# Layer 2's channel mixing: result copies on one engine, image 0 copied on chip, its first statistics split

## The chip, the cores and the metric

The kernel runs on one core of a Trainium2 chip. The metric is device time in microseconds; three runs of the kernel before gave 5497.55 to 5502.83, median 5501.04. TensorE (PE) multiplies matrices from SBUF into PSUM, VectorE (DVE), ScalarE (ACT) and GpSimd (POOL) work elementwise, and SyncE (SP) issues most of the transfers (DMAs). Each engine runs its own instructions in order, and engines wait for each other through semaphores.

## The reference

Four layers, each `x = x + f(norm(x))`, on 8 images of 56 x 56 positions and 192 channels. The change lies in layer 2, between its mixing and the layer norm behind it:

```python
proj = jnp.einsum('bhwd,dc->bhwc', x, W_in) + b_in           # 384 channels
local = depthwise 3x3 convolution of proj
lr, rl = ema_scan(local, 3), its mirror image                # s = 0.6 s + 0.4 x
tb, bt = ema_scan(local, 2), its mirror image
mixed = 0.25 * (lr + rl + tb + bt) + local
mu, var = mean and variance of mixed over the 384 channels
normed = (mixed - mu) * jax.lax.rsqrt(var + LN_EPS) * ln_g + ln_b
return jnp.einsum('bhwc,cd->bhwd', normed, W_out) + b_out
```

## The kernel before, in words

**Mixing** (`layer2_mix`, L1060 to L1153) runs over 24 groups of 16 channels, all 8 images at once. A group's convolution matrices `wt` and its inputs `zc` come from memory, two groups deep. Within a group the work goes in steps of four channels, with two halves:

- `front` (L1091): 16 matmul records on PE make the convolution in PSUM (`cv`, L1097, two buffers). ACT copies it to `loc` (L1105) and writes `rows`, the same with its two halves of partitions exchanged and scaled (L1108). POOL adds `loc` to `rows` (L1112). DVE makes the running sums along the image's height, downward (L1114) and upward (L1115), each a scan over 64 partitions. `loc` and `sums` have six buffers, `rows` three.
- `back` (L1120): 8 matmul records multiply `loc` and `sums` by a constant matrix (L1124), which adds the sums along the width, into PSUM (`mx`, two buffers of two halves). The first half of a buffer is copied into `yc` by DVE (L1133), the second by ACT (L1135).

A step works on the back half of one group and the front half of the next; the loop runs to 25 so that the last group's back halves stand alone at the end. When the four back halves of a group are done, SP stores `yc` for each of the 8 images into the image's buffer `md` in memory (L1151). For image 0, POOL then issues a load of the same channels back from `md[0]` into the tile `ml[0]` (L1152, called `first` there). `ml[0]` thus fills up during the mixing, while the other images are loaded whole later (`layer2_load`, L1155).

In this stage the order of instructions on each engine is chosen by the scheduler. It puts, on each engine, the back half of a step ahead of its front half: on DVE two scans and then the copy of an earlier product, on ACT the copy, then `loc` and `rows`. On SP the eight stores of a group stand ahead of the loads of a later one. From L1583 on, DVE's order is the written one.

**Behind the mixing** image 0 is normalised in groups of 8 columns of `ml[0]`, four of each half. `scaled(0, k, 0)` (L1588) takes the statistics of each column over the 384 channels (`ln_pieces`, bn_stats, L200), combines the two partial statistics into mean and variance with six small instructions (`ln_var`, L209 to L214), and makes scale and shift (`ln_rows`: a square root on ACT, L222, a reciprocal and a product on DVE, L223 and L224). `layer2_scaled` (L1160) applies them on DVE (L1167) and ACT (L1169), `layer2_turned` transposes on PE (L1178), `layer2_out` multiplies by `W_out` (L1191) and adds the residual tile `x2o` on DVE (L1196). While image 0 is worked on, SP loads the residuals (L101) and the mixed channels of image 1 (L1157), whose statistics DVE begins in the last third of image 0's work; these loads stand on SP behind the last group's stores.

Of the kernel before, what the change touches and what calls it, by code (L numbers as in the profile page):

```python
# [10 lines left out]
F32 = mybir.dt.float32  # L11
AF = mybir.ActivationFunctionType
ALU = mybir.AluOpType
# [4 lines left out]
B, H, W, C = 8, 56, 56, 192  # L18
# [24 lines left out]
C2 = 384  # L43
# [13 lines left out]
CG2 = 16  # L57
# [5 lines left out]
PH = NPAIR // 2  # L63
# [18 lines left out]
def _reversed(ap):  # L82

    dims = [list(d) for d in ap.ap]
    step, num = dims[-1]
    return bass.AP(ap.tensor, ap.offset + (num - 1) * step, dims[:-1] + [[-step, num]])
# [3 lines left out]
def kernel(ctx: ExitStack, tc: tile.TileContext, a: dict, out: bass.AP):  # L90
    nc = tc.nc
    nimg = a["x"].shape[0]
# [14 lines left out]
    def resident(name, eng=nc.sync, pool=const):  # L107
        t = pool.tile(list(a[name].shape), F32, name=name + "_sb", bufs=1)
        eng.dma_start(t, a[name])
        return t  # L110
# [10 lines left out]
    eps5 = const.tile([128, 1], F32, name="eps5")  # L121
# [28 lines left out]
    md = [dram.tile([2 * W, C2, NPAIR], F32, name=f"md{b}") for b in range(nimg)]  # L150
# [47 lines left out]
    def ln_pieces(st, yl, ns):  # L198
        for n in ns:
            nc.vector.bn_stats(st[:, n], yl[:, :, n])  # L200
# [13 lines left out]
        nc.vector.scalar_tensor_tensor(var, d, 0.25, var, ALU.mult, ALU.add)  # L214
        return mean, var

    def ln_rows(mean, var, eps, pool):

        P, A, n = var.shape
        new = lambda name: pool.tile([P, A, NPAIR // A], F32, name=name)[:, :, 0:n]  # L220
        rs, mr = new("ln_rs"), new("ln_mr")
        nc.scalar.activation(rs, var, AF.Sqrt, bias=eps[0:P])  # L222
        nc.vector.reciprocal(rs, rs)  # L223
        nc.vector.scalar_tensor_tensor(mr, mean, -0.5, rs, ALU.mult, ALU.mult)  # L224
        return rs, mr

    def in_quarters(st):
# [2 lines left out]
    def in_halves(st):  # L230
        return st.rearrange("p (s n) k -> p s n k", s=2)
# [543 lines left out]
    def layer1_norm(b, x, pool, psum, consts, first=False):  # L775
# [93 lines left out]
        for g in range(4):  # L869
            scaled(g)  # L870
            yield
# [189 lines left out]
    def layer2_mix(first):  # L1061

        band = a["band2"]
        with ExitStack() as st:
            pool = st.enter_context(tc.tile_pool(reuse_waits="tile", name="mx", bufs=2))
            psum = st.enter_context(tc.tile_pool(reuse_waits="tile", name="mxp", bufs=2, space=PSUM))
            ema = resident("ema", nc.gpsimd, pool)  # L1070
            NG = nimg * NPAIR
            dec = pool.tile([128, CG2 * nimg, NPAIR], F32, name="dec2", bufs=1)
            nc.gpsimd.memset(dec, 0.36)
            nc.gpsimd.memset(dec[:, :, 0:1], 0.0)
            dec = dec.rearrange("p c n -> p (c n)")

            def load(g):
                cs = slice(g * CG2, (g + 1) * CG2)
                wt = pool.tile([128, CG2, 256], F32, name="wt2")
                src = bass.AP(band.tensor, band.offset + g * CG2 * BL2, [[1, 128], [BL2, CG2], [1, 256]])  # L1080

                n, queues = (CG2, (nc.sync,)) if g else (4, (nc.sync, nc.gpsimd, nc.scalar))
                nc.sync.dma_start(wt[:, 0:n], src[:, 0:n])
                zc = pool.tile([128, nimg, CG2, P2], F32, name="zc2")
                for b in range(nimg):
                    queues[b % len(queues)].dma_start(zc[:, b], pd[b][:, cs])
                if n < CG2:
                    nc.sync.dma_start(wt[:, n:CG2], src[:, n:CG2])
                return wt, zc

            def front(c4, wt, zc):  # L1091

                ps = psum.tile([128, 2, 512], F32, name="cv2")
                for i in range(4):
                    dst = ps[:, i // 2, NG * (i % 2):NG * (i % 2 + 1)].rearrange("p (b n) -> p b n", n=NPAIR)
                    for q in range(2):
                        nc.tensor.matmul(  # L1097
                            dst, wt[:, c4 + i, 128 * q:128 * q + 128], zc[:, :, c4 + i, q:q + NPAIR],
                            start=(q == 0), stop=(q == 1),
                        )  # L1100
                loc, rows, sums = (
                    pool.tile([128, 4 * NG], F32, name=z, bufs=n) for z, n in (("loc", 6), ("rows", 3), ("sums", 6))
                )
                pair = lambda z: z.rearrange("p (j z) -> p j z", j=2)
                nc.scalar.copy(pair(loc), ps[:, :, 0:2 * NG])  # L1105

                for r in range(2):
                    nc.scalar.activation(  # L1108
                        pair(rows)[64 * r:64 * r + 64], ps[64 - 64 * r:128 - 64 * r, :, 0:2 * NG], AF.Identity,
                        scale=1.0 / 0.6,  # L1110
                    )
                nc.gpsimd.tensor_tensor(rows, rows, loc, ALU.add)  # L1112
                d = dec[:, 0:4 * NG]
                nc.vector.tensor_tensor_scan(sums[64:128], d[64:128], rows[64:128], 0.0, ALU.mult, ALU.add)  # L1114
                nc.vector.tensor_tensor_scan(  # L1115
                    _reversed(sums[0:64]), d[0:64], _reversed(rows[0:64]), 0.0, ALU.mult, ALU.add
                )
                return loc, sums

            def back(c4, yc, loc, sums):  # L1120
                ps = psum.tile([2 * W, 2, 512], F32, name="mx2")
                for i in range(2):
                    for k, z in enumerate((loc, sums)):
                        nc.tensor.matmul(  # L1124
                            ps[:, i, 0:2 * NG], ema[:, k],
                            z[:, 2 * NG * i:2 * NG * (i + 1)],
                            start=(k == 0), stop=(k == 1),
                        )
                for i in range(2):
                    src = ps[:, i, 0:2 * NG].rearrange("p (c b n) -> p b c n", c=2, n=NPAIR)  # L1130
                    dst = yc[:, :, c4 + 2 * i:c4 + 2 * i + 2]
                    if i == 0:
                        nc.vector.tensor_copy(dst, src)  # L1133
                    else:
                        nc.scalar.copy(dst, src)  # L1135


            loaded, now, n = [load(0)], None, C2 // CG2
            for g in range(n + 1):
                if g + 1 < n:  # L1140
                    loaded.append(load(g + 1))
                yc = pool.tile([2 * W, nimg, CG2, NPAIR], F32, name="yc2") if g else None
                following = []
                for c4 in range(0, CG2, 4):
                    if g:
                        back(c4, yc, *now.pop(0))
                    if g < n:
                        following.append(front(c4, *loaded[g]))
                if g:
                    for b in range(nimg):  # L1150
                        nc.sync.dma_start(md[b][:, (g - 1) * CG2:g * CG2], yc[:, b])  # L1151
                    nc.gpsimd.dma_start(first[:, (g - 1) * CG2:g * CG2], md[0][:, (g - 1) * CG2:g * CG2])  # L1152
                now = following  # L1153

    def layer2_load(b, pool):  # L1155
# [243 lines left out]
    with ExitStack() as st:  # L1399
        pool = st.enter_context(tc.tile_pool(reuse_waits="tile", name="qv", bufs=2))  # L1400
# [6 lines left out]
        rows, masks = [], []  # L1407
# [39 lines left out]
    with ExitStack() as st:  # L1447
        pool = st.enter_context(tc.tile_pool(reuse_waits="tile", name="mix", bufs=2))
# [24 lines left out]
    with ExitStack() as st:  # L1473
        pool = st.enter_context(tc.tile_pool(reuse_waits="tile", name="l1", bufs=2))
# [77 lines left out]
    with ExitStack() as st:  # L1552
        xpool = st.enter_context(tc.tile_pool(reuse_waits="tile", name="l2x", bufs=2, side="right"))
        pool = st.enter_context(tc.tile_pool(reuse_waits="tile", name="l2i", bufs=2))
# [16 lines left out]
    with ExitStack() as st:  # L1571
        mpool = st.enter_context(tc.tile_pool(reuse_waits="tile", name="l2m", bufs=1, side="right"))
        ml = [mpool.tile([2 * W, C2, NPAIR], F32, name="ml")]
        layer2_mix(ml[0])
        pool = st.enter_context(tc.tile_pool(reuse_waits="tile", name="l2o", bufs=2))
# [7 lines left out]
        st.enter_context(tc.manual_schedule(engines={mybir.EngineType.DVE}))  # L1583
        stat = lambda: pool.tile([2 * W, NPAIR, 6], F32, name="ln_st")
        rows, own, steps, ready, y = [None], stat(), iter(()), None, None

        def scaled(b, k, s):

            if b:
                return layer2_scaled(k, s, ml[b], *rows[0], 4 * k, pool)  # L1590
            if s == 0:
                ns = slice(4 * k, min(4 * k + 4, PH))
                ln_pieces(own, ml[0], [PH * r + n for r in range(2) for n in range(ns.start, ns.stop)])
                rows[0] = ln_rows(*ln_var(in_halves(own)[:, :, ns], C2, pool), eps5, pool)
            return layer2_scaled(k, s, ml[0], *rows[0], 0, pool)
# [5 lines left out]
        for n in range(-1, len(groups)):  # L1601
            b, k = groups[n] if n >= 0 else (-1, 0)
# [8 lines left out]
            for j in range(3):  # L1611
# [4 lines left out]
                if n >= 0:  # L1616
                    layer2_out(k, j, y, x[b], psum, w_out)
                    i = 3 * k + j
# [16 lines left out]
    with ExitStack() as st:  # L1635
# [5 lines left out]
        pool = st.enter_context(tc.tile_pool(reuse_waits="tile", name="l3o", bufs=2))  # L1641
# [135 lines left out]
```

## Time and profile before

| what | us |
|---|---|
| median of three runs | 5501.04 |
| profiled execution / its span | 5505.7 / 5503.9 |
| first convolution of the mixing | 3231.9 |
| last scan of the mixing begins | 3834.4 |
| last stores issued from | 3843.5 |
| first statistics of image 0 begin | 3850.3 |
| first scaled rows of image 0 begin | 3858.2 |

Mean durations in the mixing, in ns, with their number:

| instruction | count | mean |
|---|---|---|
| PE convolution cv, L1097 | 1536 | 355 |
| PE product mx from loc / from sums, L1124 | 384 / 384 | 553 / 544 |
| ACT loc, L1105 | 96 | 911 |
| ACT rows, L1108 | 192 | 912 |
| POOL addition, L1112 | 96 | 2326 |
| DVE scan, L1114 / L1115 | 96 / 96 | 2039 / 2901 |
| DVE copy, L1133 | 96 | 590 |
| ACT copy, L1135 | 96 | 532 |
| POOL issue of ml<-md, L1152 | 24 | 537 |

All times of the trace count from the start of the span. In lists of waits, "A <- B" means that A stood idle until B was done. Matmuls overlap, so the mean of one is longer than the distance to the next: two products of 448 columns start 0.75 us apart per pair. "PEld" is the load of weights into PE, which runs beside its matmuls.

### The profile page before, as it was taken

To read this page: it belongs to the slowest core of one execution; us is meant where nothing else is said; L and a number is where in the kernel's file an instruction comes from. 1 tells how busy PE (TensorE), PEld (TensorE's weight loads), DVE (VectorE), ACT (ScalarE), POOL (GpSimd) and SP (SyncE) were. 2 spreads that over 40 slices of the span, in tenths; PEclk is the share of its full clock that TensorE was granted. 3 is DMA by queue.
4 is the path that set the end of the run, shared out by engine and by line. 5 is a ranking of instruction groups with operands and counts; after the bars stand their busy time and mean duration, and the time that the engine had idled before them with its cause. 6 is when DMAs were issued, how large, how long until landed. Compare 5 with 4: busy or idle time off the path is not lost. (4 is left out here: it accounts for less than half of the span.)

```text
span 5503.9 us, 113538 instructions
## 1 busy us (share of the span) xinstructions
PE 4998.8 (91%) x49428; PEld 3379.9 (61%) x49428; DVE 3053.1 (55%) x4273; ACT 2311.1 (42%) x3109; POOL 1877.9 (34%) x1583
## 2 busy tenths in 40 slices
PE   7999969999999979999987989998798787999999
PEld 6778866666666645666665757775344586444444
DVE  4555533555555456666666868888777214343331
ACT  3444435555555434444441025554576302333333
POOL 5555555555555434344431023333011101001000
PEclk9999989999999989999998999999899898999999
DMA  5989896777777623223225757675777696212211
GB/s 148 234 222 232 222 269 261 272 273 275 277 276 272 201 68 85 77 81 86 82 59 156 270 214 235 230 237 188 182 218 220 241 340 235 65 61 87 70 40 27
DMA packets 533335, 1002.87 MB, mean 182 GB/s; under 512 B 256104, under 2 KB 467812, under 8 KB 501460
## 3 DMA queue, kind: packets, MB, share of 16 engines
q1 hardware_dynamic: 519984, 945.58, 53.5%
q0 software_dynamic: 8576, 40.69, 2.3%
q10 hardware_dynamic: 4276, 9.32, 0.6%
q8 instruction: 389, 6.37, 0.5%
q14 instruction: 110, 0.90, 0.1%
HBM read 665.22 MB, written 346.75 MB: 184 GB/s over the span
## 5 line engine op out<-in xcount | busy, mean ns | idle before, releaser
L465 POOL COPY lc<-lt 128x896 f32<-128x896 f32 (+1 forms) x320 | 616.4, 1934 | 513.9 <-PE op L473 490.7
L432 PE MATMUL qv<-w_qv_sb,x 64*112 64x256 f32 (+1 forms) x5376 | 692.0, 410 | 24.0 <-DVE act L438 20.1
L432 PEld LDWEIGHTS qv<-w_qv_sb,x 64*112 64x112 f32 x5376 | 592.5, 176 | 112.5 <-DVE act L438 32.2
L438 DVE TENSOR_TENSOR act<-qv,b_qv 112x640 f32<-112x640 f32 x448 | 318.7, 752 | 325.4 <-PE qv L432 238.5
L442 ACT ACTIVATE act<-act 112x640 f32<-112x640 f32 x448 | 300.3, 683 | 414.3 <-DVE act L438 403.7
L408 POOL TENSOR_TENSOR qv<-act 112x320 f32<-112x320 f32 x448 | 346.5, 799 | 288.9 <-ACT act L442 193.6
L473 PEld LDWEIGHTS op<-rc,lc 128*56 128x56 f32 x9216 | 329.6, 135 | 124.2 <-issue 65.9
L1366 PE MATMUL ph<-y,w_sb 64*128 64x392 f32 x2304 | 398.9, 499 | 6.5 <-ACT hid L1370 6.5
L473 PE MATMUL op<-rc,lc 128*56 128x56 f32 x9216 | 354.5, 221 | 55.1 <-ACT rc L465 38.2
L1377 PE MATMUL po<-hid,w_sb 128*64 128x392 f32 x2304 | 386.3, 494 | 0.0
L1384 DVE TENSOR_TENSOR x<-x,z 128x392 f32<-128x392 f32 x96 | 72.8, 759 | 520.3 <-ACT z L1382 520.3
L1097 PE MATMUL cv<-zc,wt 128*128 128x224 f32 x1536 | 312.8, 355 | 24.9 <-DMA zc<-pd 24.2
L1097 PEld LDWEIGHTS cv<-zc,wt 128*128 128x128 f32 x1536 | 290.3, 189 | 68.3 <-issue 53.1
L1366 PEld LDWEIGHTS ph<-y,w_sb 64*128 64x128 f32 x2304 | 220.7, 189 | 176.5 <-issue 26.5
L506 PE MATMUL y<-pp,w_o_sb 128*64 128x392 f32 x1536 | 309.0, 499 | 5.8 <-DVE pp L500 5.8
L1112 POOL TENSOR_TENSOR rows<-rows,loc 128x896 f32<-128x896 f32 x96 | 223.3, 2326 | 261.9 <-ACT rows L1108 204.6
L483 PE MATMUL pj<-xn,w_p_sb 64*128 64x392 f32 x1536 | 289.1, 509 | 19.7 <-ACT pp L490 18.1
L924 POOL TENSOR_TENSOR e<-e,mx 128x1176 f32<-128x1176 f32 x64 | 140.2, 2190 | 462.6 <-DVE mx L923 398.3
L465 ACT COPY rc<-rt 128x896 f32<-128x896 f32 (+1 forms) x160 | 279.9, 1749 | 40.0 <-DMA rt<-right 40.0
L1377 PEld LDWEIGHTS po<-hid,w_sb 128*64 128x64 f32 x2304 | 162.7, 137 | 213.8 <-issue 213.8
L500 DVE TENSOR_TENSOR pp<-pp,ot 128x784 f32<-128x784 f32 x128 | 124.1, 970 | 292.6 <-PE ot L495 239.9
L1115 DVE TENSOR_TENSOR_SCAN sums<-dec,rows 64x896 f32<-64x896 f32 x96 | 278.5, 2901 | 1.3
(252 smaller groups left out, 9194.8 us busy)
## 6 DMA issues: line engine op xcount, KB each, us to landing
lt<-left SPq DMA_DIRECT2D x72, 1792.0 KB
rt<-right SPq DMA_DIRECT2D x72, 1792.0 KB
left<-qv SPq DMA_DIRECT2D x224, 252.0 KB
right<-qv SPq DMA_DIRECT2D x96, 504.0 KB
wt<-in_band_dram SPq DMA_DIRECT2D x23, 2048.0 KB
zc<-pd SPq DMA_DIRECT2D x187, 232.0 KB
pd<-pt SPq DMA_DIRECT2D x7, 5568.0 KB
bm<-bmask SPq DMA_DIRECT2D x64, 588.0 KB
```

The source lines that it names most:

```text
L408: nc.gpsimd.tensor_tensor(qv[:, s, s0:s1, k], *(acts[s][:, which, 0:n].rearrange("p (s d) -> p s d", d=64) for which in range(2)), ALU.mult,)
L432: nc.tensor.matmul(ps[s][:, which, 0:n], x[64 * s:64 * s + 64, j, bass.ts(i, 2 * W)], w_qv[64 * s:64 * s + 64, j, which, 64 * s0:64 * s1], ...
L438: nc.vector.tensor_tensor(acts[s][:, :, 0:n], ps[s][:, :, 0:n], b_qv[:, :, 64 * s0:64 * s1], ALU.add)
L442: nc.scalar.activation(acts[s][:, :, 0:n], acts[s][:, :, 0:n], AF.Silu)
L465: copy(c[:, 0:nu], raw.rearrange("p (w u d) -> p u d w", u=nu, d=64 // nu)[:, :, d0:d0 + 8])
L473: nc.tensor.matmul(op[64 * u:64 * u + W, i, :], lc[:, u, i], rc[:, u, i], start=True, stop=True)
L483: nc.tensor.matmul(ps[:, s, 0:TT], w_p[64 * s:64 * s + 64, j, 128 * c:128 * c + 128], xn[64 * s:64 * s + 64, j, bass.ts(t, TT)], start=(j ...
L506: nc.tensor.matmul(y[64 * s:64 * s + 64], w_o[:, 2 * g + u, 64 * j:64 * j + 64], pp[:, u, s], start=(u == 0), stop=(u == 1),)
L1097: nc.tensor.matmul(dst, wt[:, c4 + i, 128 * q:128 * q + 128], zc[:, :, c4 + i, q:q + NPAIR], start=(q == 0), stop=(q == 1),)
L1115: nc.vector.tensor_tensor_scan(_reversed(sums[0:64]), d[0:64], _reversed(rows[0:64]), 0.0, ALU.mult, ALU.add)
L1366: nc.tensor.matmul(ps[:, s, 0:TT], w0[64 * s:64 * s + 64, j, m * 128:(m + 1) * 128], y[64 * s:64 * s + 64, j, ts], start=(j == 0), stop=(j ...
L1377: nc.tensor.matmul(ps[64 * s:64 * s + 64], w1[:, m, 64 * j:64 * j + 64], hid[:, m, s], start=(m == 0), stop=(m == 5),)
```

## The change

Both halves of a result are copied out of PSUM by ACT; DVE's copy is gone. For image 0, SP transfers the channels from `yc` straight into `ml[0]`, ahead of the seven stores of the other images; `md[0]` and POOL's load are no longer used. The statistics of image 0's first 8 columns are taken in two parts: over the first 368 channels as soon as DVE has done its last scan and those channels are there, and over the last 16 channels once they have arrived; bn_aggr combines both parts of a column. It gives the mean itself, not twice the mean, and so `ln_rows` has a factor to be given. The other columns are handled as before.

```diff
-    def ln_rows(mean, var, eps, pool):
+    def ln_rows(mean, var, eps, pool, share=-0.5):
...
-        nc.vector.scalar_tensor_tensor(mr, mean, -0.5, rs, ALU.mult, ALU.mult)
+        nc.vector.scalar_tensor_tensor(mr, mean, share, rs, ALU.mult, ALU.mult)
...
                 for i in range(2):
                     src = ps[:, i, 0:2 * NG].rearrange("p (c b n) -> p b c n", c=2, n=NPAIR)
-                    dst = yc[:, :, c4 + 2 * i:c4 + 2 * i + 2]
-                    if i == 0:
-                        nc.vector.tensor_copy(dst, src)
-                    else:
-                        nc.scalar.copy(dst, src)
+                    nc.scalar.copy(yc[:, :, c4 + 2 * i:c4 + 2 * i + 2], src)
...
                 if g:
-                    for b in range(nimg):
+                    nc.sync.dma_start(first[:, (g - 1) * CG2:g * CG2], yc[:, 0])
+                    for b in range(1, nimg):
                         nc.sync.dma_start(md[b][:, (g - 1) * CG2:g * CG2], yc[:, b])
-                    nc.gpsimd.dma_start(first[:, (g - 1) * CG2:g * CG2], md[0][:, (g - 1) * CG2:g * CG2])
...
+        early = pool.tile([2 * W, 8, 12], F32, name="ln_early", bufs=1)
+        for n in range(8):
+            nc.vector.bn_stats(early[:, n, 0:6], ml[0][:, 0:C2 - CG2, PH * (n // 4) + n % 4])
...
-            if s == 0:
+            if s == 0 and k == 0:
+                for n in range(8):
+                    nc.vector.bn_stats(early[:, n, 6:12], ml[0][:, C2 - CG2:C2, PH * (n // 4) + n % 4])
+                both = pool.tile([2 * W, 2, 4, 2], F32, name="ln_mv", bufs=1)
+                for n in range(8):
+                    nc.vector.bn_aggr(both[:, n // 4, n % 4], early[:, n])
+                rows[0] = ln_rows(both[:, :, :, 0], both[:, :, :, 1], eps5, pool, -1.0)
+            elif s == 0:
```

## The prediction

> **What bounds the kernel now.** I read the page first, then the chain that ended last, then the stretches of the mixing stage, its waits, and the instructions in order of time. On the page TensorE is the busy engine of the whole program, and the chain that ended last walks through this stage's end:
>
> ```profile
> PE 4998.8 (91%) x49428; PEld 3379.9 (61%) x49428; DVE 3053.1 (55%) x4273; ACT 2311.1 (42%) x3109; POOL 1877.9 (34%) x1583
> ```
>
> The mixing stage runs from about 3220 to 3859 us. Busy time by stretch (us of PE, PEld, DVE, ACT, POOL, then granted clock, DMA share, GB/s) shows two different regimes:
>
> ```profile
> 3300.00:3800.00 500.00, 497.88 (x1931) 352.74 (x1930) 437.12 (x241) 254.22 (x322) 196.72 (x101) 1.00 0.70 233
> 3800.00:3837.00 37.00, 31.77 (x107) 19.61 (x106) 32.61 (x21) 16.44 (x22) 12.05 (x7) 0.95 0.30 98
> 3837.00:3859.00 22.00, 4.74 (x8) 1.91 (x8) 9.00 (x20) 2.59 (x5) 6.64 (x7) 0.66 0.67 175
> ```
>
> For 500 us PE is full and VectorE (DVE) 87% full; then come 22 us in which PE works 4.7. The chain names what fills those 22 us (start, length, what):
>
> ```profile
> 3837.50 4.75 PE mx L1124 x8
> 3843.49 2.19 DMA md<-yc
> 3846.22 3.97 DMA ml<-md
> 3850.26 6.14 DVE ln_st L200 x8
> 3858.23 2.67 ACT yt L1169 x3
> ```
>
> Everything here is in series: last product, one transfer out, one back, eight statistics, first scaled rows.
>
> A busy PE can still lose time. The waits of 3300 to 3800 (us in total, times, longest):
>
> ```profile
> ACT yc L1135 <- DVE yc L1133: 240.8, 80, 5.7
> PEld mx L1124 <- ACT yc L1135: 12.8, 34, 1.4
> ```
>
> and two steps (a step is four channels of convolution and four of result):
>
> ```profile
> 3503.04 0.59 DVE L1133 COPY yc<-mx 112x448 f32<-112x448 f32 x1
> 3503.67 0.53 ACT L1135 COPY yc<-mx 112x448 f32<-112x448 f32 x1 [4.63 <-DVE yc L1133]
> 3504.25 1.01 PE L1124 MATMUL mx<-loc,ema_sb 128*112 128x448 f32 x2
> 3507.35 3.24 PE L1097 MATMUL cv<-zc,wt 128*128 128x224 f32 x16
> 3510.43 0.91 PE L1124 MATMUL mx<-loc,ema_sb 128*112 128x448 f32 x2
> 3511.59 2.08 POOL L1112 TENSOR_TENSOR rows<-rows,loc 128x896 f32<-128x896 f32 x1 [1.99 <-ACT rows L1108]
> 3511.67 3.87 DVE L1115 TENSOR_TENSOR_SCAN sums<-dec,rows 64x896 f32<-64x896 f32 x1
> 3513.43 3.24 PE L1097 MATMUL cv<-zc,wt 128*128 128x224 f32 x16
> 3516.09 2.02 DVE L1114 TENSOR_TENSOR_SCAN sums<-dec,rows 64x896 f32<-64x896 f32 x1
> 3519.77 3.24 PE L1097 MATMUL cv<-zc,wt 128*128 128x224 f32 x16
> ```
>
> The convolutions start 6.08 us apart, then 6.34. In the long step the product at 3504.25 had to wait until ScalarE's copy freed its PSUM buffer (there are two), and that copy stood behind DVE's copy, which stood behind two scans. So PE alone needs 6.08 us a step, and the copy chain adds 0.25 to every other one.
>
> **The change, part by part.** The order of instructions on PE is unchanged. On DVE 96 copies go, on ScalarE 96 come, on GpSimd (POOL) 24 DMA issues go, and on SyncE (SP) the first of each group's eight stores goes to the tile instead of memory. Only the first statistics block behind the stage differs beyond that.
>
> *Copies to ScalarE, long stretch.* ScalarE gains 96 x 0.53 us: 254 busy us of 500 become about 297, 3.8 us of a step. Queued behind its two copies are loc (0.91) and the two rows (1.83), and POOL and the scans wait for those. The two copies (1.06) fit beside the convolution (3.1 us), loc and rows beside the next product (3.0 us), so I cost them at nothing; without that cover each would add its 0.53 to the step. DVE loses 0.59 a step. With the copy no longer behind the scans, the PSUM wait of PE goes. From the convolution at 3250.55 to the last at 3817.62 there are 91 steps in 567.1 us; at 6.08 they would take 553.3, an excess of 13.8. The first of these steps (7.51 instead of 6.08, it waits for sums) keeps its 1.4, so at most 12.4 can go. The surely attributed part is about 35 waits x 0.25 = 8.8. I take 10.
>
> What is late next is the pair DVE and POOL. A step then holds two scans and one POOL addition, and they get in each other's way: the scan that starts 0.08 after the addition takes 3.87 instead of 2.02. In the trace that makes 2.04 + 3.87 = 5.9 us a step, under 6.08; while the stage fills, where they collide all the time, addition plus scan repeat every 3.75 us, so 3.75 + 2.04 = 5.8. The Trainium skill, "SBUF — State Buffer" (SBUF: two separate sides), speaks against the change: a DVE instruction with two SBUF inputs and a GpSimd one that reads SBUF exclude each other for the whole instruction. By that the step would be 2.08 + 2 x 2.04 = 6.16 us and only (6.23 - 6.16) x 90 = 6 us could go. The rows show about 0.2 to 0.3 us of each collision overlapped, so I follow the rows: PE stays the bound.
>
> *The tail.* Durations of before, from the last convolution at 3817.62: it ends 3820.86; loc and rows 2.8, to 3823.7; POOL 2.1, to 3825.85; two scans 4.1, to 3829.95 (before, 3836.37, since each of these engines was one or two steps behind the copies). PE meanwhile finishes the earlier products without waiting; the last one, 8 matmuls at 0.375, ends at 3832.95 (before 3842.2). Two copies on ScalarE in a row, 1.1: 3834.05. Before, the first store was issued at 3843.49: 9.4 us are gone.
>
> *Copy on chip.* The trace has no SBUF to SBUF transfer. Nearest is md<-yc of the same 196 KB: issued 3843.49, waiter free at 3846.22, 2.7 us. Bounds: 2.2 (its own piece in the chain) and 6.7 (both legs, no gain). I take 2.7: landed 3836.75. The leg ml<-md, 4.0 us, is gone. SP's number of issues is the same; behind the first stand seven stores. POOL loses 24 issues of 0.54 and the waits ahead of them, off the path; behind the last of them stood the load of w_out and a 4.6 us clearing of zq, which now come earlier than they are needed (before, w_out was issued at 3846.77 and first used at 3863.5).
>
> *Statistics in two parts.* Eight early bn_stats take 6.1 us as before (they read 368 of 384 channels). They wait for the transfers of groups 0 to 22, the last issued near 3819, and stand behind the last scan: 3829.95 to 3836.1. The gap between that scan and the last landing is 6.8, so they are hidden; uncovered they would cost up to 6.1. Then eight bn_stats of 16 values: small DVE instructions here take 0.09 to 0.20 each, so 0.7 to 1.6, taken 1.2. Eight bn_aggr of 12 values: from 0.1 each (a small instruction) to 0.47 (the row of bn_aggr of 72 values), 0.8 to 3.8; nearer the small ones, taken 2.4. Six small instructions of the old variance go, 1.0. Square root, reciprocal and shift stay, 0.8. First scaled rows: 3836.75 + 1.2 + 2.4 + 0.8 = 3841.2, before 3858.23: 17.0 earlier.
>
> *What is late next.* Image 0's residual and image 1's mixed channels are loaded by SP behind the stores, so they come only 9.4 us earlier, plus about 1 for the transfers taken out of the way. By the trace's DMA packets they were complete near 3864 and 3884; DVE first used them at 3870.98 and 3889.26. They now land near 3854 and 3873.5 and are wanted at 3854 and 3872.3. So 1.3 us come back, and the tail is worth about 15.5.
>
> Sum: 10 + 15.5 = 25.5 us. The profiled execution took 5505.7 (span 5503.9), so it would take about 5480; the median of the three runs is 5501.04, 0.08% below it, so 5475.5.
>
> **The rivals.**
> 1. *The port paces the long stretch* (17%). For it: that the scan nearly doubles in a collision, and that every step would now collide instead of every second. Against: 5.9 is below 6.08. The stretch gives 0 to 6 and the tail 15.5: about 5483.
> 2. *Everything comes* (10%). The loads do not hold image 0 up and PE keeps its full clock there (before, it was granted half speed from 3858 to 3878, after the idle stretch): 12 + 18: 5470.
> 3. *Little comes* (8%). The on-chip transfer is no faster than the two legs, the early statistics are not covered, or the copies hold ScalarE up: the tail gives 9, the stretch nothing: 5492.
> 4. *Slower* (5%). Both scans of each step are stretched by POOL, as in the filling of the stage (3.73 and 3.75). A step of 7.5 us would add 1.3 x 90 = 115 us: near 5600. It decides from a step of about 6.4 us (0.17 x 90 = 15.5, the tail's gain). Against it: one addition a step can stretch only one scan.
>
> That the change doesn't do what it says is not among them: on each engine the instruction order shows the moves.
>
> **How the numbers follow.** My forecast has 60% and covers 5469 to 5484; the likeliest value is 5475.5. To hold 8 in 10 the range takes in rivals 1 and 2: 5466 to 5489. A measurement of this kernel tells about 0.2%, 11 us, from no change. Faster by more: 60 + 17 + 10 and a third of rival 3, 90%. Same 5%, slower 5%.
>
> **What would show it.** Convolution starts all 6.08 apart and no PE wait for ScalarE's copy (stretch right); 6.16 or more with PE idle is rival 1. Last scan to first scaled rows about 11 us instead of 22. The transfer ml<-yc 2 to 3 us. Statistics: no wait of early ones, eight aggregates about 2.4. After it, a DVE wait of 1 to 2 us for image 1's channels. The forecast is wrong if the step stays at 6.2, or if image 0 waits for its loads by more than 5 us.

## The result, and the profile after

Six runs of the changed kernel gave 5469.26 to 5481.53 us, median 5473.73; six of the kernel before had a median of 5501.48. The ratio is 0.9949 (95% interval 0.9936 to 0.9962), so about 28 us are gone, 21 to 35 by the interval. The profiled execution took 5471.44 us, its span 5469.3: 34 us less than the profiled one of before. Some 8 of those 34 lie ahead of the mixing (its fifth convolution starts at 3242.57 instead of 3250.55), where nothing was changed; kernels that are equal up to there differ by as much (3238.66 in e4_no_early, 3251.20 in e5_no_chip). So I count from that convolution on.

The page's first line, and the busy time by stretch (columns as before: us of PE, PEld, DVE, ACT, POOL, then granted clock, DMA share, GB/s):

```profile
PE 4981.5 (91%) x49428; PEld 3382.6 (62%) x49428; DVE 2944.8 (54%) x4187; ACT 2362.1 (43%) x3205; POOL 1872.9 (34%) x1559
```

```profile
3300.00:3800.00 500.00, 500.00 (x1977) 363.83 (x1976) 346.24 (x167) 303.11 (x410) 190.17 (x83) 1.00 0.67 221
...
3837.00:3859.00 22.00, 16.53 (x70) 6.59 (x69) 13.54 (x26) 8.37 (x11) 0.00 (x0) 0.84 0.95 220
```

PE was full before and is full now, but the 500 us hold 1977 matmul records instead of 1931. That is how a gain shows on an engine that is "full": more records in the same time. VectorE (DVE) is busy 91 us less there (some 47 for its 80 copies, the rest because its scans are shorter, as shown below), ScalarE (ACT) 49 us more. The last stretch, nearly empty before, now holds work of image 0. The waits of 3300 to 3800 (us in total, times, longest):

```profile
POOL rows L1112 <- ACT rows L1108: 307.7, 82, 4.0
ACT loc L1105 <- PE cv L1097: 172.9, 82, 2.1
DVE sums L1114 <- POOL rows L1112: 152.4, 76, 2.0
ACT yc L1131 <- PE mx L1124: 20.8, 82, 0.3
```

No PE wait for a copy is left; everybody waits for PE, directly or one after the other. A step in order of time:

```profile
3499.62 0.97 ACT L1131 COPY yc<-mx 112x448 f32<-112x448 f32 x2 [0.25 <-PE mx L1124]
...
3501.61 2.02 DVE L1114 TENSOR_TENSOR_SCAN sums<-dec,rows 64x896 f32<-64x896 f32 x1 [2.02 <-POOL rows L1112]
...
3503.62 1.83 ACT L1108 ACTIVATE rows<-cv 64x896 f32<-64x896 f32 x2
3503.65 2.02 DVE L1115 TENSOR_TENSOR_SCAN sums<-dec,rows 64x896 f32<-64x896 f32 x1
...
3505.51 3.24 PE L1097 MATMUL cv<-zc,wt 128*128 128x224 f32 x16
3505.58 2.08 POOL L1112 TENSOR_TENSOR rows<-rows,loc 128x896 f32<-128x896 f32 x1 [4.01 <-ACT rows L1108]
...
3511.59 2.67 PE L1097 MATMUL cv<-zc,wt 128*128 128x224 f32 x13
```

Steps are 6.08 us, every one but the first (7.51, as before). And POOL's addition lies between the scans: it meets only the last 0.09 us of a second scan, and the next first scan begins when it is done. Now the tail:

```profile
3797.43 3.24 PE L1097 MATMUL cv<-zc,wt 128*128 128x224 f32 x16
...
3809.79 5.95 DVE L1584 BATCH_NORM_STATS2 ln_early<-ml 112x6 f32<-112x368 f32 x8
3813.72 0.52 SPq L1146 DMA_DIRECT2D ml<-yc  x1
3816.78 0.80 DVE L1592 BATCH_NORM_STATS2 ln_early<-ml 112x6 f32<-112x16 f32 x8 [1.04 <-DMA ml<-yc]
3817.49 0.70 DVE L1595 BATCH_NORM_AGGREGATE ln_mv<-ln_early 112x2 f32<-112x12 f32 x8
3819.05 3.07 ACT L1165 ACTIVATE yt<-ml,ln_mr,ln_rs 112x384 f32<-112x384 f32 x3 [0.52 <-DMA md<-yc]
```

Between the last convolution and the first scaled rows (`yt`) lie 21.62 us. Before there were 40.61, from the line below to the first scaled rows at 3858.23:

```profile
3817.62 3.24 PE L1097 MATMUL cv<-zc,wt 128*128 128x224 f32 x16
```

(The releaser that the line of 3819.05 names is a store; by the times it is the product of L224, done at 3818.97.)

The chain that ended last has left this path:

```profile
3800.67 12.04 PE mx L1124 x32
...
3819.07 0.68 SPq L101
...
3820.62 35.14 DMA ml<-md
3855.78 3.16 DVE ln_st L200 x4
```

It now runs through SP's queue and the load of image 1's channels, issued at 3820.62 behind the last stores and the first loads of image 0's residual. DVE wants these channels 4.5 us before they are there, and it waits as long for something else before that. Its first residual addition, and its first statistics of image 1:

```profile
3835.17 0.68 DVE L1192 SCALAR_TENSOR_TENSOR x2o<-po,vecs_sb,x2o 128x448 f32<-128x448 f32 x1 [4.51 <-PE po L1187]
...
3855.78 3.16 DVE L200 BATCH_NORM_STATS2 ln_st<-ml 112x6 f32<-112x384 f32 x4 [4.50 <-DMA ml<-md]
```

The first of these waits is put down to the product `po`, which was ready sooner: PE's ten products before it ended at 3830.57, and in e4_no_early the addition follows these ten at once. In e0_after_again, the same kernel once more, it is put down to image 0's residual:

```profile
3838.85 0.68 DVE L1192 SCALAR_TENSOR_TENSOR x2o<-po,vecs_sb,x2o 128x448 f32<-128x448 f32 x1 [3.48 <-DMA x2o<-x]
```

In the trace of after, too, the residual's second load reports its end at 3835.04, just ahead of the addition. So image 0 waits for two loads that stand behind the last stores: 4.5 us for its residual and 4.5 for image 1's channels (3.5 and 5.6 in e0_after_again).

### The profile page after: what moved, and what is told of

The parts are those of the page before. It is cut to its first block, busy times and chain, and to the rows that moved or that the text cites. A ratio compares the mean times of both kernels' runs of the same rounds, so it can differ in the third digit from the quotient of the medians.

```text
span 5469.3 us, 113665 instructions
## 1 busy us (share of the span) xinstructions
PE 4981.5 (91%) x49428; PEld 3382.6 (62%) x49428; DVE 2944.8 (54%) x4187; ACT 2362.1 (43%) x3205; POOL 1872.9 (34%) x1559
## 3 DMA queue, kind: packets, MB, share of 16 engines
q1 hardware_dynamic: 519984, 945.58, 53.9%
## 4 chain that ended last, share of the span: by engine, by line
PE 73%; DVE 11%; ACT 5%; DMA 4%; issue 3%; POOL 2%; SPq 1%; ACTq 0%; DVEq 0%; POOLq 0%
PE qv L432 10%; PE po L1373 7%; PE ph L1362 7%; PE mx L1124 5%; PE cv L1097 5%; PE pj L483 5%; PE pin L1044 4%; PE y L506 4%; PE qk_ps L886 4%; PE op L473 3%; PE po L1187 3%; PE v_ps L901 3%; PE cps L1265 3%; DVE ln_st L200 2%; PE ot L495 2%
## 5 line engine op out<-in xcount | busy, mean ns | idle before, releaser
L1362 PEld LDWEIGHTS ph<-y,w_sb 64*128 64x128 f32 x2304 | 220.4, 189 | 176.4 <-issue 26.1
L1114 DVE TENSOR_TENSOR_SCAN sums<-dec,rows 64x896 f32<-64x896 f32 x96 | 206.1, 2147 | 188.7 <-POOL rows L1112 188.1
```

Source lines behind the costliest of these rows:

```text
L1362: nc.tensor.matmul(ps[:, s, 0:TT], w0[64 * s:64 * s + 64, j, m * 128:(m + 1) * 128], y[64 * s:64 * s + 64, j, ts], start=(j == 0), stop=(j ...
```

## The experiments

My theory (A): the copies give the stretch and most of the tail; the copy on chip and the early statistics make image 0 start sooner, but image 1's load, tied to the last store, then holds image 0's end, so that they give little. The rival (B): the three parts add up.

For every run I took three times from its trace: the stretch (fifth to last convolution, 91 steps), the tail (last convolution to the first scaled rows) and image 0 (from these to its last residual addition). Their sum is free of what differs upstream; but it comes from one trace of each kernel, and it leaves out what follows image 0 (from there to image 7's last addition all these kernels take 386.9 to 388.9 us, e6_residual_early 390.8). The runs were made on several chips; each ratio is to the kernel before on the same chip.

| run | median us | ratio to before (interval) | stretch | tail | image 0 | sum, against before |
|---|---|---|---|---|---|---|
| before | 5501.48 | | 567.07 | 40.61 | 71.28 | 678.96 |
| after | 5473.73 | 0.9949 (0.9936–0.9962) | 554.86 | 21.62 | 76.49 | -26.0 |
| e0_after_again | 5475.36 | 0.9954 (0.9942–0.9966) | 554.86 | 21.60 | 76.47 | -26.0 |
| e1_scalar_only | 5476.18 | 0.9967 (0.9955–0.9980) | 554.87 | 31.01 | 70.44 | -22.6 |
| e2_chip_only | 5494.86 | 0.9996 (0.9987–1.0004) | 565.85 | 36.58 | 70.82 | -5.7 |
| e3_early_only | 5495.83 | 0.9999 (0.9990–1.0009) | 565.49 | 33.09 | 73.06 | -7.3 |
| e4_no_early | 5469.63 | 0.9948 (0.9936–0.9960) | 554.86 | 27.65 | 70.34 | -26.1 |
| e5_no_chip | 5476.64 | 0.9954 (0.9941–0.9967) | 554.86 | 25.66 | 72.21 | -26.2 |
| e6_residual_early | 5471.47 | 0.9951 (0.9939–0.9963) | 554.87 | 22.66 | 73.11 | -28.3 |
| e8_vector_copies | 5493.65 (one run; before, once there, 5491.67) | | 565.25 | 28.44 | 72.36 | -12.9 |
| e9_swapped | 5576.03 | 1.0142 (1.0128–1.0156) | 645.60 | 40.53 | 71.49 | +78.7 |
| e10_after_swapped | 5487.67 | 0.9977 (0.9968–0.9987) | 562.29 | 30.19 | 72.43 | -14.0 |

**One part alone.** e1_scalar_only is the kernel before with both copies on ACT:

```diff
-                    dst = yc[:, :, c4 + 2 * i:c4 + 2 * i + 2]
-                    if i == 0:
-                        nc.vector.tensor_copy(dst, src)
-                    else:
-                        nc.scalar.copy(dst, src)
+                    nc.scalar.copy(yc[:, :, c4 + 2 * i:c4 + 2 * i + 2], src)
```

> The kernel before with only the copies moved to ScalarE. By the chip of the first four runs and the trace of the changed kernel: the long stretch gives 12.2 us (steps of 6.08 instead of 6.23), the last copy ends 9.6 us sooner after the last convolution, and nothing behind it changes, so image 1's channels are not waited for: 21.8 us faster than the kernel before, some 4 us short of the changed kernel. If instead POOL's DMA issues hold the long stretch up as well, steps stay above 6.08 and the gain is under 15 us.

Measured: 554.87 for the stretch and 9.6 off the tail, 22.6 of the 26.0 us. Channels still travel through memory, POOL still issues its loads, and the stretch is the same to 0.01 us: those issues cost it nothing here.

e2_chip_only has only the transfer from `yc`, e3_early_only only the two-part statistics; each leaves the copies as before:

```diff
-                    for b in range(nimg):
+                    nc.sync.dma_start(first[:, (g - 1) * CG2:g * CG2], yc[:, 0])
+                    for b in range(1, nimg):
                         nc.sync.dma_start(md[b][:, (g - 1) * CG2:g * CG2], yc[:, b])
-                    nc.gpsimd.dma_start(first[:, (g - 1) * CG2:g * CG2], md[0][:, (g - 1) * CG2:g * CG2])
```

> The kernel before with only the copy on chip. If the long stretch is held up by the copy chain alone: steps stay at 6.2 us and the tail is shorter by the leg taken out, 3.7 us in all. If POOL's issues and its waits for the stores matter for the stretch: steps between 6.08 and 6.2, up to 12 us more.

> The kernel before with only the split statistics. Eight early ones fit into the 7.4 us in which DVE waited for the transfer, so the first scaled rows come 5.7 us sooner; before, image 1's channels landed about 5 us ahead of their use, so all of it but 0.5 stays: 5 us faster. If those channels land later than I read from the packets, DVE waits for them and less is left.

Measured: both shorten the tail (by 4.0 and 7.5) and leave the steps, the odd first one apart, at 6.20 us each (before 6.22). The timed runs can't tell either from before; the intervals reach from 7 us faster to 2 slower, and from 5 faster to 5 slower. The 7.3 us that e3_early_only gains in the table are more than its timed runs allow; the table is good for which part does what, not for a microsecond or two. So the stretch belongs to the copies alone.

**One part undone.** e4_no_early is the kernel after with the old statistics, e5_no_chip the kernel after with stores and POOL loads of image 0 as before; e0_after_again is the kernel after once more, beside them.

```diff
e4_no_early
-        early = pool.tile([2 * W, 8, 12], F32, name="ln_early", bufs=1)
-        for n in range(8):
-            nc.vector.bn_stats(early[:, n, 0:6], ml[0][:, 0:C2 - CG2, PH * (n // 4) + n % 4])
...
-            if s == 0 and k == 0:
...
-            elif s == 0:
+            if s == 0:
```

> The changed kernel with the statistics of image 0's first columns taken in one piece again (copies on ScalarE and the copy on chip stay). Its own gain in the trace: from the first late statistics to the first scaled rows 2.3 us instead of 8.0, so 5.7. Theory A, image 1's channels cap the tail: those loads are tied to the last store, so the 5.7 us are spent waiting for them, and without the early statistics the program takes the same time as the changed kernel (within 1.5 us), with DVE's wait for image 1's channels going from about 5.7 to about 0. Rival B, the parts add up: 5.7 us slower than the changed kernel, and the wait for image 1's channels stays.

> The changed kernel with image 0's channels stored to memory and loaded back by POOL again (copies on ScalarE and the split statistics stay). The leg taken out is worth 3.7 us in the trace (last store to first statistics 6.8 us before, 3.1 after). Theory A, capped by image 1's loads: same time as the changed kernel within 1.5 us, the wait for image 1's channels shrinking from about 5.7 to about 2. Rival B, the parts add up: 3.7 us slower. Rival C, POOL's DMA issues were part of what held the long stretch up: a step longer than 6.08 us in the long stretch, each 0.1 us being 9 us.

> The changed kernel once more, on the chip of the three others, as their measure: 0.9949 of the kernel before (0.9936 to 0.9962).

Measured: without the early statistics the tail is 6.0 longer and image 0 is 6.2 shorter; without the copy on chip the tail is 4.0 longer and image 0 4.3 shorter. The sums agree within 0.3 us and the three medians within 7 us, with intervals that overlap. In e4_no_early DVE waits for neither load. So by these traces each part adds about 3.5 us to e1_scalar_only and both together no more: B falls, A stands, though image 1's load is not alone in it. Against e4_no_early, image 0 of the kernel after loses 6.2 us: 1.7 by its fourth residual addition, behind the wait for the residual, and 4.5 at image 1's load.

**Take the cap away.** e6_residual_early is the kernel after with image 0's residual loaded during the mixing, so that image 1's load follows the last stores directly in SP's queue (room for it comes from a shorter `dec` and one `loc` buffer less). The lines that time this load and give the later residuals one buffer each are left out here:

```diff
-            dec = pool.tile([128, CG2 * nimg, NPAIR], F32, name="dec2", bufs=1)
+            dec = pool.tile([128, 4 * nimg, NPAIR], F32, name="dec2", bufs=1)
...
-                    pool.tile([128, 4 * NG], F32, name=z, bufs=n) for z, n in (("loc", 6), ("rows", 3), ("sums", 6))
+                    pool.tile([128, 4 * NG], F32, name=z, bufs=n) for z, n in (("loc", 5), ("rows", 3), ("sums", 6))
...
+                if g == 6:
+                    residual(following[-1][0][:, 0:1])
```

> The changed kernel with image 0's residual (2.4 MB) loaded during the mixing, in about the seventh group, instead of behind the last stores; to make room the scans' constant tile is a quarter as long and loc has five buffers. Theory A: image 1's channels then stand first behind the stores and land 8 us earlier, so the wait of about 5.7 us for them goes and the program is about 5 us faster than the changed kernel (near 5468 where that takes 5473). Rival B: they do not set the end; no change within 1.5 us. Either way up to 2 us can be lost in the group in which the residual is loaded.

Measured: DVE's waits for both loads are gone, as wanted, but most of the gain is not there. Image 0 takes 73.11, not the 70.3 to 70.4 of the runs without a wait, and the stretch from image 0's end to image 7's takes 390.8 instead of 387.2 (perhaps because the residual tiles have one buffer each there, which wasn't tried). Part of the 2.7 us can be seen in the granted clock. First e4_no_early, then e6_residual_early, each from its first scaled rows on:

```profile
3821.00:3831.00 10.00, 8.29 (x30) 4.46 (x32) 9.37 (x19) 7.58 (x11) 0.00 (x0) 0.60 1.06 226
...
3871.00:3881.00 10.00, 10.00 (x46) 4.02 (x45) 10.00 (x15) 3.55 (x7) 0.00 (x0) 0.71 0.62 142
```

```profile
3823.60:3833.60 10.00, 8.48 (x27) 4.27 (x28) 9.46 (x20) 7.68 (x10) 1.16 (x4) 0.52 1.14 283
...
3873.60:3883.60 10.00, 9.57 (x32) 3.56 (x33) 8.99 (x14) 4.70 (x8) 0.00 (x0) 0.63 0.56 138
```

In both stretches PE was granted less (0.52 against 0.60, 0.63 against 0.71) and finished fewer records (27 against 30, 32 against 46). Why it was granted less there wasn't tried. So the 5 us that were expected aren't shown: the table has 2.3 us against the kernel after, the stretch behind image 0 takes them back, and the timed runs (5471.47 against 5475.36 of e0_after_again, with overlapping intervals) can't tell the two kernels apart. That the loads hold image 0 up rests on the waits in the traces and on e4_no_early and e5_no_chip.

**Is the pair POOL and DVE near its limit?** e7_half_conv leaves out half of each convolution's matmuls, so PE is out of the way:

```diff
-                    for q in range(2):
+                    for q in range(1):
...
-                            start=(q == 0), stop=(q == 1),
+                            start=True, stop=True,
```

> The changed kernel with half of the convolution's matmuls left out (the second of two shifts of the input), so that PE needs about 4.6 us a step instead of 6.08. What paces the step then: if DVE and POOL exclude each other for whole instructions, as the skill has it, 2.08 + 2 x 2.04 = 6.16 us, slower than now, or 6.08 with the 0.09 us of overlap seen now, so no gain at all; if a collision overlaps by 0.2 to 0.3 us, as the rows of the kernel before showed, 5.8 to 5.9 us and 17 to 25 us less; if they don't bind, ScalarE (3.7 us) or PE paces and the step is near 4.7, 125 us less.

One run took 5461.25 (before, on that chip, 5498.28). The busy times and waits of 3300 to 3780:

```profile
3300.00:3780.00 480.00, 392.70 (x1297) 235.64 (x1298) 476.39 (x163) 299.16 (x406) 205.11 (x81) 0.98 0.69 229
```

```profile
PEld mx L1124 <- DVE sums L1115: 135.9, 76, 3.0
...
ACT rows L1108 <- DVE sums L1115: 79.8, 59, 2.1
```

```profile
3331.54 3.90 POOL L1112 TENSOR_TENSOR rows<-rows,loc 128x896 f32<-128x896 f32 x1 [3.94 <-ACT rows L1108]
3331.55 2.02 DVE L1115 TENSOR_TENSOR_SCAN sums<-dec,rows 64x896 f32<-64x896 f32 x1
...
3333.59 3.73 DVE L1114 TENSOR_TENSOR_SCAN sums<-dec,rows 64x896 f32<-64x896 f32 x1
```

Now DVE is the full engine (476 of 480 us) and others wait for its scans. 81 additions in 480 us make 5.93 us a step; half of them follow at 6.01 or 6.02. By the times the two engines take turns. The addition and a scan begin together at 3331.5; the scan takes its usual 2.02, and the addition ends 1.87 us behind it (alone it takes 2.08). The next scan begins at 3333.59 and ends 1.88 us behind the addition (alone 2.02). So each turn saves 0.14 to 0.21 us, and the step stays below the 6.16 that exclusion for the whole instruction would give, though not by much.

**What the copies did to the stretch.** So far I had held that DVE's copy cost the stretch because it stands behind two scans. e8_vector_copies puts both copies there, in the kernel after:

```diff
-                    nc.scalar.copy(yc[:, :, c4 + 2 * i:c4 + 2 * i + 2], src)
+                    nc.vector.tensor_copy(yc[:, :, c4 + 2 * i:c4 + 2 * i + 2], src)
```

> The changed kernel with both copies of a result on DVE instead of both on ScalarE; on-chip copy and early statistics kept. DVE's instructions of a step are then two scans and two copies: 2 x 2.04 + 2 x 0.59 = 5.3 us with no collision, and 1.9 more for each scan that POOL's addition stretches, 7.2. If what held the stretch before was a copy standing behind the scans on DVE (my account), two of them there bring the step back to more than the 6.23 of before, about 6.3 to 7.2 us, and the kernel takes 5480 to 5570. If what mattered was that two engines shared the two halves of a result, so that each waited for the other, one engine for both is as good here as there: a step of 6.08 to 6.1, and 5470 to 5476.

```profile
3272.17 1.80 PE L1124 MATMUL mx<-loc,ema_sb 128*112 128x448 f32 x2 [7.53 <-DVE yc L1131]
...
3502.90 3.24 PE L1097 MATMUL cv<-zc,wt 128*128 128x224 f32 x16
...
3502.97 2.08 POOL L1112 TENSOR_TENSOR rows<-rows,loc 128x896 f32<-128x896 f32 x1 [4.00 <-ACT rows L1108]
3502.98 1.12 DVE L1131 COPY yc<-mx 112x448 f32<-112x448 f32 x2
...
3508.98 3.24 PE L1097 MATMUL cv<-zc,wt 128*128 128x224 f32 x16
```

The first account falls: with twice the copies on DVE the step is 6.08 too. The stretch is longer (565.25) only by one step of 16.47 while it fills, in which PE waits 7.5 us for a copy that stands behind slow scans; and the tail is 6.8 longer than after: the last copy comes 4.2 later, and the early statistics now stand behind the copies. The time, 5493.65, lies in the first account's range, but not for its reason, and one run says little: 25 runs of before on one chip spread over 18 us.

What both fast kernels share is that no copy of ACT waits for DVE. The trace of before shows what such a wait does; these lines stand between the steps that the prediction shows:

```profile
3504.09 0.91 ACT L1105 COPY loc<-cv 128x896 f32<-128x896 f32 x1
...
3505.02 1.83 ACT L1108 ACTIVATE rows<-cv 64x896 f32<-64x896 f32 x2
...
3506.93 0.54 POOL L1152 DMA_DIRECT2D ml<-md  x1 [5.69 <-ACT rows L1108]
...
3507.49 2.11 POOL L1112 TENSOR_TENSOR rows<-rows,loc 128x896 f32<-128x896 f32 x1
...
3509.63 2.02 DVE L1114 TENSOR_TENSOR_SCAN sums<-dec,rows 64x896 f32<-64x896 f32 x1 [1.40 <-POOL rows L1112]
...
3515.47 0.59 DVE L1133 COPY yc<-mx 112x448 f32<-112x448 f32 x1
```

It is a ring. DVE's copy at 3503.04 releases ACT's copy (0.63 later), behind which stand `loc` (0.42) and `rows` (0.93); POOL's addition follows (2.47, with an issue of its load in between), then a scan (2.14), a second scan (2.04), and the next DVE copy behind that one, stretched by POOL's next addition (3.80). That this comes to the 12.43 us between two DVE copies is only adding up; what makes it a ring is that each link begins as soon as the one before lets it, so that no slack is left anywhere. Where POOL issues no load, its addition itself is longer (2.62 beside a scan instead of 2.11), and the lap from 3515.47 to 3527.88 takes 12.41. PE needs 12.16 for two steps. In e2_chip_only, which has no such loads, all steps from the sixth on alternate 6.33 and 6.09, 12.42 a pair. In before and e3_early_only, which have them, the pattern is disturbed in a few places, each time by a longer step with some of 6.08 behind it. In before all 91 steps, less the 1.43 us of their odd first one, take 565.64, 6.216 each. (That this equals 12.43 / 2 so closely is chance.) So the ring paced the stretch, not PE with an occasional wait.

To test it, two kernels cut the ring but leave a copy on DVE: ACT takes the first half of a result, DVE the second. DVE's copy then waits for ACT's, and ACT's for PE alone. e9_swapped does this to the kernel before, e10_after_swapped to the kernel after:

```diff
                     if i == 0:
+                        nc.scalar.copy(dst, src)
+                    else:
                         nc.vector.tensor_copy(dst, src)
-                    else:
-                        nc.scalar.copy(dst, src)
```

> The kernel before with one thing changed: ScalarE copies the first half of a result and DVE the second, so that DVE's copy waits for ScalarE's and no longer the other way round. No copy is taken from DVE; copy on chip and early statistics are left out. If the stretch was held by a ring (DVE's copy, then ScalarE's copy, loc, rows, POOL's addition, two scans, DVE's copy again, which the trace of before shows closing in 12.42 us for two steps), the ring is cut here, since ScalarE waits for PE alone: steps of 6.08, a stretch of 553 to 556 us instead of 567, and 10 to 12 us less than before from it. If what held it was DVE's copy standing behind two scans, it stands there still and waits longer: 6.2 or more a step, no gain. At the end DVE's copies still follow the scans, so that the tail gains at most 3 us by either.

> The changed kernel, but with the second half of each result copied by DVE behind ScalarE's copy of the first half; copy on chip and early statistics kept. By the ring the stretch stays at 555 us (6.08 a step), since ScalarE waits for nobody but PE. At the end the last copy again stands behind the last scans on DVE, but the products it copies end later than these, so it costs under 1 us, and ScalarE's last copy is taken off the path; the early statistics stand behind DVE's copies: 0 to 6 us later. Cover of image 1's load as in the kernel after: 5471 to 5480. If DVE's work itself slows the stretch, 6.2 a step and 5485 or more.

e10_after_swapped, two convolutions:

```profile
3489.98 3.24 PE L1097 MATMUL cv<-zc,wt 128*128 128x224 f32 x16
3490.06 0.59 DVE L1135 COPY yc<-mx 112x448 f32<-112x448 f32 x1
3490.06 2.08 POOL L1112 TENSOR_TENSOR rows<-rows,loc 128x896 f32<-128x896 f32 x1 [4.01 <-ACT rows L1108]
3490.18 0.53 ACT L1133 COPY yc<-mx 112x448 f32<-112x448 f32 x1 [0.25 <-PE mx L1124]
...
3496.07 3.24 PE L1097 MATMUL cv<-zc,wt 128*128 128x224 f32 x16
```

Apart from the filling (one step of 13.51, which makes the stretch 562.29 and which I had not expected) every step is 6.08 with a copy still on DVE: the ring is what counts. (This run and e8_vector_copies begin with one long step, which shifts the engines against each other; that they would settle at 6.08 without it isn't shown. In before, steps of 6.08 after a disturbance give way to 6.34 again within ten steps.) Its tail is 8.6 longer than after (30.19 against 21.62), more than expected: the last copy comes 22.1 us after the last convolution instead of 16.3, not under 1 us later, and the early statistics stand behind it.

e9_swapped missed altogether: 75 us slower than before, where the ring account gave 10 to 12 less and the other no gain. The waits of 3300 to 3800:

```profile
POOL ml L1152 <- DMA md<-yc: 162.7, 16, 11.8
...
PEld mx L1124 <- DVE yc L1135: 54.5, 23, 4.5
PE mx L1124 <- DVE yc L1135: 46.6, 16, 4.1
```

Here POOL's load of image 0's channels does harm. In this order of instructions it reaches the head of POOL's queue up to 11.8 us before the store that it reads is done, and the addition that the scans need stands behind it; the scans starve, DVE's copies with them, and PE, which waits for those copies, stands idle for 46.6 of the 500 us (453.41 busy). e10_after_swapped has no such load and none of these waits. As e9_swapped alone therefore doesn't test the ring, the test is e10_after_swapped. The rest of the difference between the two, the early statistics, lies behind the stretch.

## Why the prediction was right, and where it was not

| step | predicted | measured |
|---|---|---|
| stretch | -10 (8.8 to 12.4) | -12.2 |
| last copy, after the last convolution | 16.4 (9.4 sooner) | 16.3 (9.6 sooner) |
| transfer on chip, issue to DVE | 2.7 (2.2 to 6.7) | 3.06 |
| early statistics | hidden | hidden, 5.95 |
| late statistics, 8 bn_stats, to the first bn_aggr | 1.2 (0.7 to 1.6) | 0.71 |
| 8 bn_aggr | 2.4 (0.8 to 3.8) | 0.70 |
| root, reciprocal, shift | 0.8 | 0.86 |
| first scaled rows sooner | 17.0 | 19.0 |
| given back in image 0 | 1.3 (17.0 less 15.5: 1.5 in the sum) | 5.2 |
| sum | -25.5 | -26.0 |

The tail was right in its order, and each row but the bn_aggr within half a microsecond or so; each was a duration from the trace of before or stood between bounds from it. That the sum agrees to half a microsecond is luck: the stretch gave 2.2 us more and image 0 began 2.0 sooner than said, and image 0 gave back 3.7 more. The eight bn_aggr took the price of the smallest DVE instructions, below the low bound, not a share of the row with 72 values, and so image 0 started 2 us earlier than I said. That earlier start was then lost. Image 1's channels were there 58.4 us after the last convolution instead of the estimated 55.9, and wanted at 53.9 instead of 54.7, which makes the wait 4.5 instead of 1.3. The residual was costed at nothing, since it was to land when it is wanted, at 36.4; it landed at 37.6 and was wanted at 33.2. The prediction had named both loads as what is late next, and got their order and place right; but by its own mark, a wait of more than 5 us for them, this part of it failed: the two waits are 9.0 us, and image 0 took 5.2 longer than before. e4_no_early and e5_no_chip show that this is a cap: 4 to 6 us less in the tail bring nothing.

In the stretch the size was right and the mechanism half so. The prediction saw that ACT's copy stood behind DVE's and DVE's behind scans, and that both go; it priced this as 35 waits of PE. What was there was the ring of 12.43 us for two steps, which gives the whole excess: 91 x (6.216 - 6.08) = 12.4 us, of which the runs show 12.2 gone. One sentence was wrong: that every step would now collide. By the order of the lines it is the ring that put POOL's addition beside a scan. Mean ns of the second scan, 3300 to 3780, before and after:

```profile
L1115 DVE TENSOR_TENSOR_SCAN sums<-dec,rows 64x896 f32<-64x896 f32 x78 | 225.5, 2891 | 1.0
```

```profile
L1115 DVE TENSOR_TENSOR_SCAN sums<-dec,rows 64x896 f32<-64x896 f32 x80 | 173.6, 2170 | 1.1
```

Without it POOL adds while DVE waits, and the scans run at nearly their own length. So rival 1 (the port) did not come true, and even where nearly all collide, as in e7_half_conv, the step is 5.93. The margin is thin, though. The prediction's 5.9 leaves out the 0.08 us by which the addition begins ahead of the scan; a step in which one addition meets one scan takes 6.01 to 6.02 there, 0.06 below PE's 6.08. Still, its choice of the rows (5.8 to 5.9) over the rule of the Trainium skill, "SBUF — State Buffer" (SBUF: two separate sides), by which the step is 6.16, was right: the two engines do hold each other up, but for a little less than the whole instruction.

The prediction also costed POOL's 24 loads at nothing. That holds in the orders of before and after (e1_scalar_only and after have the same stretch). In the order of e9_swapped it would have been wrong by some 83 us (a stretch of 645.60 against 562.29 in e10_after_swapped). And one reading of rival 2 was wrong: before, PE was granted 0.51 from 3858 to 3868, but 1.00 from 3868 to 3878, not half speed up to there.

Open: the 8 us ahead of the mixing, why PE was granted less in e6_residual_early, and what a kernel without both waits for loads, and with nothing else changed, would gain.

## What to carry to other kernels

When two engines share the pieces of one result and one piece waits for the other, follow the waiting engine's queue: if what stands behind that wait feeds the engine that is waited for, and each link begins as soon as the one before ends, it is a ring, and the sum round it, divided by the steps it spans, is the pace, even where PE looks full. Give all pieces to the engine that waits for PE alone. When a tail is shortened, look at once at the next loads that are tied to the same last store: beyond their slack further cuts bring nothing, as two parts here did that each saved 4 to 6 us and together gained no more than one.

## What was not expected of the hardware

- bn_aggr over 12 values: eight in 0.70 us, 0.09 each. bn_stats over 16 strided values: eight in 0.80 us, 0.10 each.
- A 196 KB transfer from SBUF to SBUF: 3.06 us from issue to DVE going on, against 2.7 for the store of the same bytes to memory before.
- A POOL addition and DVE scans in each other's way take turns (e7_half_conv): the addition 3.90 us instead of 2.08 behind one scan, the next scan 3.73 instead of 2.02 behind the addition, with 0.14 to 0.21 us saved at each turn.
